# A cross-attention mask carried by the last row of the keys

## The chip, the core and the metric

One core of a Trainium2 chip runs the whole kernel. The time is the device time of one execution, in microseconds; the figure for a kernel is the median of several runs. The profile is of one further execution. The engines are named as the profile names them: PE is TensorE (PEld its weight loads), DVE is VectorE, ACT is ScalarE, POOL is GpSimd, SP is SyncE, which here only issues DMAs.

## What is computed

The input is 8 batches of 256 rows with 128 features, and a context of 64 rows with 64 features for each batch. Four stages follow one another: a memory attention with 16 heads (L0), a small cross-attention (L1), six identical transformer layers (L2), and a last attention with a layer norm (L3). All is in 32-bit floats. Nearly all of the time goes to L2, and the change is in its cross-attention:

```python
def _mha(s, t, kv_w, q_w, o_w, o_b, mask):
    k, v = jnp.split(s @ kv_w, 2, axis=-1)
    q = t @ q_w
    ...
    scores = jnp.einsum('bhqd,bhkd->bhqk', q, k) * D ** (-0.5)
    scores = jnp.where(mask[:, None] == 0, jnp.float32(-1000000000.0), scores)
    attn = jax.nn.softmax(scores, axis=-1)
    ...

def step(t, p):
    tn = _ln(t, norm_g, norm_b)
    t = _mha(tn, tn, skv, sq, sow, sob, tgt_mask) + t     # self-attention, 256 keys
    tn = _ln(t, norm_g, norm_b)
    t = _mha(src, tn, ckv, cq, cow, cob, src_mask) + t    # cross-attention, 64 keys
    tn = _ln(t, pg, pb)
    t = t + (jax.nn.relu(tn @ w1 + b1) @ w2 + b2)
```

`src` is the context, the same in all six layers, and `src_mask` is one row of 64 flags for each batch. 16 heads of 64 features are used.

## The kernel before

The kernel is one long program without loops on the chip. Its order is written out by hand: `at(tick, phase, fn)` puts a step into a plan, and at the end (L1307 to L1323) the plan is gone through by tick and, within a tick, by phase. Every instruction of the four compute engines is tied to stand behind the one before it on its own engine. So on each engine the instructions run in the order of the plan, and an instruction that waits holds up all that stand behind it on its engine. DMAs on SP's queue are not tied in this way.

In each layer self-attention takes four ticks a batch (`plan_sa`), then cross-attention two ticks a batch (`plan_ca`), one for each half of 128 query rows. `T_ca` is the tick at which a layer's cross-attention begins; below, "tick n" of a layer means `T_ca + n`, so batch b has its two score blocks in ticks 2b and 2b+1, for b = 0 to 7. The feed-forward part (`plan_ff`) of batch b stands in ticks 2b+7 and 2b+9, and the next layer's self-attention projections begin in tick 12.

The pieces of cross-attention, each with its line:

- The layer norm runs ahead (`ahead`): statistics on DVE (L849 to L855, phase 6 of tick 2b-4, so in even ticks, where the feed-forward part's statistics of another batch stand too), a power on POOL (L859), the normalising on ACT (L868), a transpose on PE (L882), and a copy out of PSUM on ACT that applies scale and bias of the norm feature by feature (L884). Features are then partitions.
- The weights of queries and keys of all heads are folded together once a layer (`plan_ca_weights`): the weights are transposed on DVE (L1057), written to DRAM and fetched back regrouped (L1060, L1068), regrouped again on POOL (L1074) and multiplied on PE (L1083), which gives `AT` (with the attention's scale, L1095) and `WVO` (L1093). `T_ca - 6` is the tick it is planned from.
- `keys_both` makes the keys of two batches from `AT` and the context (L1120, ticks 4i-2, phase 3.7), copied by ACT into two buffers of the tag "q" (L1126). A key tile is 128 partitions (features of the query side) by 16 heads by 64 keys.
- `plan_weights_64`, one block of 128 query rows by 16 heads by 64 keys. In tick n: `scores` (phase 1) on PE, sixteen 128x32 matmuls (L356) and sixteen mask matmuls (L363); `lower` (phase 2): a copy on ACT (L372), the max on DVE (L374), a subtraction on POOL (L375); the exponents on ACT (L381, phase 8). In tick n+1, the sum and reciprocal on DVE (L385, L386) and the division on POOL (L387), at phase 2.4. In tick n+2 the transposes on DVE (L395, phase 2.5). In tick n+3 the output matmuls on PE (L429, phase 3.0) and the residual add on DVE (L1145).
- Values (L318 on PE, L324 on ACT) come in even ticks, phase 3.2. The feed-forward matmuls (L1161, L1178) come in odd ticks, phases 3.1 and 3.2, and the add behind the second of them (L1182) on DVE.

So within one tick DVE does, in this order, the max of this tick's block, sum and reciprocal of the block before, transposes of the one before that, the residual add of the one before that, and in even ticks statistics.

The mask is a small bf16 array `nm2` whose partition 0 holds 0 or -1e30 for each batch and key, and zeros elsewhere. `ones0` has a one only in partition 0. The mask matmul adds that row to each query row in PSUM:

```python
for a in range(4):
    nc.tensor.matmul(
        sc[32 * a : 32 * a + 32, q, :], lhsT=ones0, rhs=mask,
        start=False, stop=True,
    )
```

In self-attention (`plan_sa`) the names that come up are the scores (L939), the exponents on DVE and ACT (L953, L958), the division on POOL (L968), transposes (L978), output matmuls (L994), the copy of their result by DVE (L299), the value projection (L921), the other projections (L902), the output projection (L1012) and the add behind it (L1019). Outside of layers: L513 and L515 are small DVE instructions of L0's entropy, L631 an add of L1's values, L873 the normalising of self-attention's rows on DVE.

Of the kernel before, what the change touches and what calls it, by code (L numbers as in the profile page):

```python
# [8 lines left out]
F32 = mybir.dt.float32  # L9
# [18 lines left out]
def tile_xattn_stack(ctx: ExitStack, tc: tile.TileContext, io, out: bass.AP):  # L28
# [124 lines left out]

    norm_g = column("L2_norm_g")
    norm_b = column("L2_norm_b")
    pre_g = load_const("L2_pre_gT", [D, NL])
    pre_b = load_const("L2_pre_bT", [D, NL])
    ff_b1 = load_const("L2_ff_b1T", [P, NL, FF // P])
# [103 lines left out]
        return nm  # L262


    nm2 = const.tile([P, B, M], BF16, tag="nm2", name="nm2")
    nc.vector.memset(nm2, 0.0)
    ones0 = const.tile([P, 32], BF16, tag="ones0", name="ones0")
    nc.vector.memset(ones0, 0.0)
    nc.vector.memset(ones0[0:1], 1.0)


    def stats(xin, eps):
# [21 lines left out]
    def at(tick, phase, fn):  # L294
        plan.setdefault(tick, []).append((phase, fn))
# [30 lines left out]
        )  # L326
        return vw

    def plan_weights_64(tick, qt, qT, keys, values, mask, take):

        tl = {}

        def scores():
            sc = two_banks("sc").rearrange("p (q x) -> p q x", q=4)
            if mask is None:
                for i in range(4):
                    for a in range(4):
                        q = (i + 2 * (a // 2)) % 4  # L340
                        rows = slice(64 * (a // 2), 64 * (a // 2) + 64)
                        qb = 4 * qt + q
                        nc.tensor.matmul(
                            sc[32 * a : 32 * a + 32, q, :],
                            lhsT=qT()[rows, qb * 32 : (qb + 1) * 32],
                            rhs=keys()[rows, 4 * (a % 2) : 4 * (a % 2) + 4, :].rearrange(
                                "p h k -> p (h k)"
                            ),
                            start=True, stop=True,
                        )  # L350
                tl["sc"] = sc.rearrange("p q x -> p (q x)")
                return
            for q in range(4):
                qb = 4 * qt + q
                for a in range(4):
                    nc.tensor.matmul(  # L356
                        sc[32 * a : 32 * a + 32, q, :],
                        lhsT=qT()[:, qb * 32 : (qb + 1) * 32],
                        rhs=keys()[:, a].rearrange("p h k -> p (h k)"),
                        start=True, stop=False,  # L360
                    )
                for a in range(4):
                    nc.tensor.matmul(  # L363
                        sc[32 * a : 32 * a + 32, q, :], lhsT=ones0, rhs=mask,
                        start=False, stop=True,
                    )
            tl["sc"] = sc.rearrange("p q x -> p (q x)")

        def lower():
            sc = tl.pop("sc")  # L370
            e = big("e", shape=(P, 16, M))
            nc.scalar.copy(e.rearrange("p h k -> p (h k)"), sc)  # L372
            m = sm([P, 16], "m16")
            nc.vector.tensor_reduce(m, e, AX.X, ALU.max)  # L374
            nc.gpsimd.tensor_tensor(  # L375
                e, e, m.unsqueeze(2).to_broadcast([P, 16, M]), ALU.subtract
            )
            tl["e"] = e

        def exps():  # L380
            nc.scalar.activation(tl["e"], tl["e"], AF.Exp)  # L381

        def divide():
            r = sm([P, 16], "r16")
            nc.vector.tensor_reduce(r, tl["e"], AX.X, ALU.add)  # L385
            nc.vector.reciprocal(r, r)  # L386
            nc.gpsimd.tensor_tensor(  # L387
                tl["e"], tl["e"], r.unsqueeze(2).to_broadcast([P, 16, M]), ALU.mult
            )

        def turn():
            e = tl.pop("e").rearrange("p (q h) (k x) -> p (h k) q x", q=4, x=32)
            eT = big("k" if mask is None else "o", shape=(P, 8, 4, 32))
            for i in range(2):
                nc.vector.transpose(eT[:, 4 * i : 4 * i + 4], e[:, 4 * i : 4 * i + 4])  # L395
            tl["eT"] = eT

        def sums_by_head():

            ps = two_banks("mm").rearrange("p (i x) -> p i x", i=2)  # L400
            eT, vw = tl.pop("eT"), values()
            for i in range(2):
                for k in range(2):
                    for j in range(4):
                        nc.tensor.matmul(
                            ps[32 * j : 32 * j + 32, i, :P],
                            lhsT=cones.rearrange("p a f -> p (a f)") if i == 0
                            else vw[:, 4 * k + j, :],
                            rhs=eT[:, 2 * j + k].rearrange("p q x -> p (q x)"),
                            start=(k == 0), stop=(k == 1),  # L410
                        )
# [12 lines left out]
        def sums():  # L424
            ps = mm_tile()
            eT, vw = tl.pop("eT"), values()
            for s in range(8):
                g, r, k = s // 4, s // 2 % 2, s % 2
                nc.tensor.matmul(  # L429
                    ps[:, :D], lhsT=eT[:, s].rearrange("p q x -> p (q x)"),  # L430
                    rhs=vw[:, r, k, g, :], start=(s == 0), stop=(s == 7),
                )
            take(ps)

        at(tick, 1, scores)
        at(tick, 2, lower)
        if mask is None:
# [197 lines left out]

    def mask_keys():
        mi = big("q", dtype=I32)
        mi = mi[0:1, : B * M].rearrange("p (b m) -> p b m", b=B)
        nc.sync.dma_start(out=mi, in_=io["mask_Bx1xS2_if1"].rearrange("b o m -> o b m"))
        nc.vector.tensor_scalar(nm2[0:1], mi, 0.0, -BIG, ALU.is_equal, ALU.mult)  # L640

    mask_bf = []

# [39 lines left out]
    def plan_l0(b, T):  # L683
# [87 lines left out]
        at(T + 1, 3.2, make_values)  # L771
        for qt in range(QT):
            plan_weights_64(
                T + qt, qt, lambda: st["q"], lambda: st["k"], lambda: st["VW"], None,
                lambda ps, qt=qt: add(qt, ps),
            )
        at(T + 3, 6, moments)
# [268 lines left out]
    def plan_ca_weights(l, T):  # L1046
# [54 lines left out]
            at(T - 4 + i, -0.5, lambda i=i: fetched(i))  # L1101
        at(T + 1, 8.05, regrouped)
        at(T + 2, 3.6, folded("AT", 0, lambda c: st[1][:, :, c, :], HD ** -0.5))
        at(T + 3, 3.6, folded("WVO", 1, lambda c: W["ca", l][2][:, c, :]))

    keys_of = {}

    def plan_ca(l, b, T):
# [3 lines left out]
        def keys_both():  # L1112
# [16 lines left out]
                    )  # L1129
            keys_of[b], keys_of[b + 1] = res  # L1130

        def make_values():
            st["VW"] = values_of(b, fold["WVO"])

        def res():
            st["tb"] = residual(b, W["ca", l][3])

        ahead(b, (T - 4, 6), (T - 3, 2.95), (T - 2, 2.9), norm_g, norm_b, st)
        if b % 2 == 0:
            at(T - 2, 3.7, keys_both)  # L1140
        at(T + 2, 3.2, make_values)
        at(T + 2, 7, res)

        def add(qt, ps):
            nc.vector.tensor_add(t[:, QT * b + qt, :], ps[:, :D], st["tb"][:, qt, :])  # L1145

        for qt in range(QT):
            plan_weights_64(
                T + qt, qt, lambda: st["tT"], lambda: keys_of[b], lambda: st["VW"],
                nm2[:, b].unsqueeze(1).to_broadcast([P, 4, M]), lambda ps, qt=qt: add(qt, ps),  # L1150
            )

    def plan_ff(l, b, T, T_second, steps=None):
# [117 lines left out]
    for l in range(NL):  # L1271
        T_ca = T0 + 4 * B
        T_next = T_ca + 2 * B
        for b in range(B):
            plan_sa(l, b, T0 + 4 * b)
        plan_ca_weights(l, T_ca - 6)
        for b in range(B):
            plan_ca(l, b, T_ca + 2 * b)
            T_ff = T_ca + 2 * b + 7
# [101 lines left out]
```

## Time and profile before

| | |
|---|---|
| median of 3 runs | 2408.54 us (2406.35 to 2409.70) |
| profiled execution, its own time | 2410.29 us |
| profiled execution, span | 2408.5 us |
| mean granted clock of TensorE | 0.987 |
| mask matmuls L363 | 1536 records, 112.4 us busy, 273 ns each |
| score matmuls L356 | 3072 records, 217.0 us busy, 382 ns each |
| max L374, sum L385 (DVE) | 1217 and 1208 ns each |
| subtraction L375, division L387 (POOL) | 1902 ns each |
| ACT waiting for the mask matmuls | 25.4 us, 47 times |

Busy time of a group of matmuls is the time in which at least one of them is under way; up to eight records lie over one another, and a float matmul has two records. The profile's times are microseconds from the start of the span. In a timeline a row is a start, a length, the engine, the line, the operation, output and input, and how many instructions were merged. In the chain of waits each row is a start, a length and the instruction that the end of the program is traced back through.

### The profile page before, as it was taken

The page shows a single profiled execution, that of the slowest core. Times are in us where ns is not written, and L with a number is a line of the kernel's source. Part 1 is how long each engine was busy: PE and PEld are TensorE (multiplying, and loading weights), DVE is VectorE, ACT ScalarE, POOL GpSimd, SP SyncE. Part 2 cuts the span into 40 slices and gives each one's busy share as a digit, 9 for nine tenths or more (in the row PEclk, how much of TensorE's full clock was granted, in tenths as well). Part 3 has the DMA queues.
Part 4 walks back from the last instruction along what each step waited for, and adds up shares of the span by engine and source line. Part 5 has one row for each costly group of instructions (what it writes and reads, how often), then busy time and mean ns, then how long its engine had stood idle before and what let it go on. Part 6 is the DMA issues. An engine that isn't in the chain of part 4 may idle for free.

```text
span 2408.5 us, 100346 instructions
## 1 busy us (share of the span) xinstructions
PE 2325.2 (97%) x42564; PEld 1719.9 (71%) x42564; DVE 1872.3 (78%) x6237; ACT 1707.7 (71%) x4514; POOL 1359.1 (56%) x2231
## 2 busy tenths in 40 slices
PE   7889999999999999999999999999999999999997
PEld 4557777777777777777777777777777777777775
DVE  5677887777888767888767888767888767888775
ACT  4567777667777667778667778667778667777663
POOL 2444556754556754555764555755555765455665
PEclk9989999999999999999999999999999999999998
DMA  6000022001022001012000012000013000001000
GB/s 180 2 2 20 21 73 65 2 3 30 21 64 66 11 3 30 21 56 73 12 2 26 21 45 87 12 2 18 25 40 89 21 2 18 25 26 42 2 4 16
DMA packets 102834, 76.90 MB, mean 32 GB/s; under 512 B 8113, under 2 KB 96881, under 8 KB 102386
## 3 DMA queue, kind: packets, MB, share of 16 engines
q1 hardware_dynamic: 101794, 70.16, 10.1%
q8 instruction: 335, 5.49, 0.9%
q14 instruction: 113, 0.93, 0.1%
q10 hardware_dynamic: 592, 0.33, 0.1%
HBM read 62.07 MB, written 8.39 MB: 29 GB/s over the span
## 4 chain that ended last, share of the span: by engine, by line
PE 75%; DVE 13%; ACT 5%; POOL 4%; issue 2%; DMA 0%; SPq 0%; POOLq 0%; ACTq 0%; DVEq 0%
PE sc L939 12%; PE mm L902 12%; PE mm L994 12%; PE mm L1012 6%; PE mm L921 6%; PE mm L429 6%; PE sc L356 5%; DVE e L953 3%; PE mm L1178 3%; PE mm L1161 3%; DVE eTc L978 2%; DVE m L374 2%; POOL e L968 2%; PE mm L1120 2%; PE mm L318 2%
## 5 line engine op out<-in xcount | busy, mean ns | idle before, releaser
L968 POOL TENSOR_SCALAR e<-e,rs 128x256 f32<-128x256 f32 x1536 | 702.8, 478 | 706.3 <-DVE rs L966 696.5
L958 ACT ACTIVATE e<-e,mn 128x256 f32<-128x256 f32 x1536 | 758.6, 495 | 151.3 <-DVE mn L953 146.5
L953 DVE CUSTOM_DVE_ANT_0 e<-sc,nm 128x256 f32<-128x256 f32 x1536 | 543.1, 419 | 93.4 <-PE sc L939 92.3
L978 DVE STREAM_TRANSPOSE eTc<-e 128x512 f32<-128x512 f32 x768 | 516.2, 694 | 59.4 <-POOL e L968 58.2
L939 PE MATMUL sc<-k,q 64*32 64x256 f32 x12288 | 380.8, 383 | 2.3 <-DVE o L299 1.3
L994 PE MATMUL mm<-eTc,v 32*64 32x256 f32 x12288 | 363.4, 378 | 5.7 <-ACT AT L1095 3.3
L375 POOL TENSOR_TENSOR e<-e,m 128x1024 f32<-128x1024 f32 x112 | 213.0, 1902 | 262.1 <-DVE m L374 262.1
L994 PEld LDWEIGHTS mm<-eTc,v 32*64 32x64 f32 x12288 | 277.1, 131 | 88.5 <-issue 22.2
L939 PEld LDWEIGHTS sc<-k,q 64*32 64x32 f32 x12288 | 221.8, 107 | 125.3 <-issue 51.4
L374 DVE TENSOR_REDUCE m<-e 128x16 f32<-128x1024 f32 x112 | 136.3, 1217 | 197.0 <-ACT e L372 197.0
L958 ACT ACTIVATION_READ_ACCUMULATOR e<-e,mn 128x1 f32 x1536 | 287.9, 187 | 0.0
L356 PE MATMUL sc<-q,tT 128*32 128x256 f32 x3072 | 217.0, 382 | 3.8 <-DVE t L1019 3.2
L429 PE MATMUL mm<-v,o 128*128 128x128 f32 x1536 | 197.5, 283 | 1.9 <-DVE t L1145 1.7
L429 PEld LDWEIGHTS mm<-v,o 128*128 128x128 f32 x1536 | 183.1, 195 | 19.0 <-issue 9.1
L902 PE MATMUL mm<-tT,w_sk 128*128 128x256 f32 x768 | 189.2, 389 | 0.2 <-PE mm L994 0.2
L1012 PEld LDWEIGHTS mm<-w_sow,o 128*128 128x128 f32 x1536 | 175.1, 192 | 17.6 <-issue 12.3
L921 PE MATMUL mm<-w_sv,tT 128*32 128x256 f32 x3072 | 185.6, 382 | 0.0
L1012 PE MATMUL mm<-w_sow,o 128*128 128x128 f32 x1536 | 183.6, 278 | 1.3 <-ACT WVO L1093 1.3
L387 POOL TENSOR_TENSOR e<-e,r 128x1024 f32<-128x1024 f32 x96 | 182.6, 1902 | 0.5 <-DVE r L386 0.5
L301 ACT COPY v<-mm 128x1024 f32<-128x1024 f32 x96 | 97.1, 1012 | 115.4 <-PE mm L921 115.4
L902 PE MATMUL mm<-tT,w_sq 128*128 128x256 f32 x768 | 173.6, 379 | 0.0
L902 PEld LDWEIGHTS mm<-tT,w_sk 128*128 128x128 f32 x768 | 138.3, 190 | 44.2 <-issue 29.2
(222 smaller groups left out, 3489.4 us busy)
## 6 DMA issues: line engine op xcount, KB each, us to landing
nm<-mask_d SPq DMA_DIRECT2D x192, 128.0 KB
wd<-o SPq DMA_DIRECT2D x48, 128.0 KB
w_sk<-in_L_sa_kv_dram SPq DMA_DIRECT2D x6, 512.0 KB
w_sv<-in_L_sa_kv_dram SPq DMA_DIRECT2D x24, 128.0 KB
w_sq<-in_L_sa_q_dram SPq DMA_DIRECT2D x6, 512.0 KB
w_sow<-in_L_sa_ow_dram SPq DMA_DIRECT2D x6, 512.0 KB
w_ckv<-in_L_ca_kv_dram SPq DMA_DIRECT2D x12, 256.0 KB
w_cq<-in_L_ca_q_dram SPq DMA_DIRECT2D x6, 512.0 KB
```

Of the source, the lines that this page charges most:

```text
L356: nc.tensor.matmul(sc[32 * a : 32 * a + 32, q, :], lhsT=qT()[:, qb * 32 : (qb + 1) * 32], rhs=keys()[:, a].rearrange("p h k -> p (h k)"), ...
L375: nc.gpsimd.tensor_tensor(e, e, m.unsqueeze(2).to_broadcast([P, 16, M]), ALU.subtract)
L429: nc.tensor.matmul(ps[:, :D], lhsT=eT[:, s].rearrange("p q x -> p (q x)"), rhs=vw[:, r, k, g, :], start=(s == 0), stop=(s == 7),)
L902: nc.tensor.matmul(ps[:, i * S : (i + 1) * S], lhsT=w[:, c * P : (c + 1) * P], rhs=st["tT"], start=True, stop=True,)
L921: nc.tensor.matmul(ps[32 * a : 32 * a + 32, i, :], lhsT=st["tT"][:, kb * 32 : (kb + 1) * 32], rhs=sv[:, a].rearrange("p g x -> p (g x)"), ...
L939: nc.tensor.matmul(sc[32 * a : 32 * a + 32, r, j, :], lhsT=st["q"][g][rows, a, qb * 32 : (qb + 1) * 32], rhs=st["k"][g][rows, a, :], start ...
L953: nc.vector.tensor_tensor_reduce(e[:, i, :], sc4[:, i, :], st["nm"][:, 2 * jj + i % 2, :], -1.0, 3.0 * BIG, ALU.add, ALU.min, mn[:, i : i ...
L958: nc.scalar.activation(e[:, i, :], e[:, i, :], AF.Exp, scale=-1.0, bias=mn[:, i : i + 1], accum_out=rs[:, i : i + 1],)
L968: nc.gpsimd.tensor_scalar(e[:, i, :], e[:, i, :], rs[:, i : i + 1], 1.0, ALU.mult, ALU.mult)
L978: nc.vector.transpose(eT[:, r, :, 2 * jj : 2 * jj + 2, :], e[:, 2 * r : 2 * r + 2, :].rearrange("p j (k x) -> p k j x", x=32),)
L994: nc.tensor.matmul(ops[a // 2][r * HD : (r + 1) * HD, a % 2, :S], lhsT=st["v"][kb // 4][rows, kb % 4, (2 * g + r) * HD : (2 * g + r + 1) * ...
L1012: nc.tensor.matmul(st["ps"][:, j * D : (j + 1) * D], lhsT=st["oT"][c // 4][:, c % 4, j * P : (j + 1) * P], rhs=sow[:, c, :], start=(c == 0 ...
```

## The change

The mask no longer goes through matmuls. A layer norm's normalised features sum to zero, so the last of the 128 is minus the sum of the others, and its place can be given away: the copy out of PSUM (L884) writes a constant 1 into the last feature, with scale 0 and bias 1 there, and scale 1 and bias 0 elsewhere. The norm's scale and bias move into the folded key weights `AT`: a new set of steps multiplies them by the scale, subtracts the last column from all others, and puts the sum of the products with the bias into the last column. The last row of a key tile then meets the constant 1, and the mask is added to it: one DVE instruction on partitions 96 to 127 for each batch of each layer, with `nm2` now zero except in partition 127. The weight folding is planned one tick earlier, from `T_ca - 7`.

```diff
+    norm_rows = const.tile([P, 2, D], F32, tag="norm_rows", name="norm_rows")
+    for i, name in enumerate(("L2_norm_g", "L2_norm_b")):
+        nc.sync.dma_start(out=norm_rows[:, i, :], in_=io[name].partition_broadcast(P))
...
-    nm2 = const.tile([P, B, M], BF16, tag="nm2", name="nm2")
-    nc.vector.memset(nm2, 0.0)
-    ones0 = const.tile([P, 32], BF16, tag="ones0", name="ones0")
...
+    nm2 = const.tile([P, B, M], F32, tag="nm2", name="nm2")
+    last_on = ident[:, P - 1 : P]
+    last_off = const.tile([P, 1], F32, tag="last_off", name="last_off")
+    nc.vector.tensor_scalar(last_off, last_on, -1.0, 1.0, ALU.mult, ALU.add)
+    last_big = const.tile([P, 1], F32, tag="last_big", name="last_big")
+    nc.vector.tensor_scalar(last_big, last_on, -BIG, None, ALU.mult)
...
                         rhs=keys()[:, a].rearrange("p h k -> p (h k)"),
-                        start=True, stop=False,
-                    )
-                for a in range(4):
-                    nc.tensor.matmul(
-                        sc[32 * a : 32 * a + 32, q, :], lhsT=ones0, rhs=mask,
-                        start=False, stop=True,
+                        start=True, stop=True,
                     )
...
     def mask_keys():
         mi = big("q", dtype=I32)
-        mi = mi[0:1, : B * M].rearrange("p (b m) -> p b m", b=B)
-        nc.sync.dma_start(out=mi, in_=io["mask_Bx1xS2_if1"].rearrange("b o m -> o b m"))
-        nc.vector.tensor_scalar(nm2[0:1], mi, 0.0, -BIG, ALU.is_equal, ALU.mult)
+        mi = mi[:, : B * M].rearrange("p (b m) -> p b m", b=B)
+        nc.sync.dma_start(
+            out=mi, in_=io["mask_Bx1xS2_if1"].rearrange("b o m -> (b o) m").partition_broadcast(P)
+        )
+        nc.vector.tensor_scalar(nm2, mi, 0.0, last_big, ALU.is_equal, ALU.mult)
...
         at(T + 2, 3.6, folded("AT", 0, lambda c: st[1][:, :, c, :], HD ** -0.5))
+
+        def rows(i):
+            return norm_rows[:, i].unsqueeze(1).to_broadcast([P, HC, D])
+
+        def meet_bias():
+            st["z"] = big("q", shape=(P, HC, D))
+            nc.gpsimd.tensor_tensor(st["z"], st["AT"], rows(1), ALU.mult)
+
+        def sum_bias():
+            st["add"] = sm([P, HC], "add")
+            nc.vector.tensor_reduce(st["add"], st.pop("z"), AX.X, ALU.add)
+
+        def scale():
+            nc.gpsimd.tensor_tensor(st["AT"], st["AT"], rows(0), ALU.mult)
+
+        def lose_last():
+            last = sm([P, HC], "last")
+            nc.gpsimd.tensor_copy(last, st["AT"][:, :, D - 1])
+            nc.gpsimd.tensor_tensor(
+                st["AT"], st["AT"], last.unsqueeze(2).to_broadcast([P, HC, D]), ALU.subtract
+            )
+
+        def put_bias():
+            nc.gpsimd.tensor_copy(st["AT"][:, :, D - 1], st.pop("add"))
+
+        at(T + 2, 8.05, meet_bias)
+        at(T + 3, 2.35, scale)
+        at(T + 3, 8.05, lose_last)
+        at(T + 3, 8.7, sum_bias)
+        at(T + 4, -0.1, put_bias)
...
     def plan_ca(l, b, T):
...
+        def mask_keys():
+            last = keys_of[b][96:].rearrange("p a c k -> p (a c) k")
+            nc.vector.tensor_tensor(
+                last, last, nm2[96:, b].unsqueeze(1).to_broadcast([32, 16, M]), ALU.add
+            )
...
-        ahead(b, (T - 4, 6), (T - 3, 2.95), (T - 2, 2.9), norm_g, norm_b, st)
+        ahead(b, (T - 4, 6), (T - 3, 2.95), (T - 2, 2.9), last_off, last_on, st)
         if b % 2 == 0:
             at(T - 2, 3.7, keys_both)
+        at(T - 1, 5, mask_keys)
...
-        plan_ca_weights(l, T_ca - 6)
+        plan_ca_weights(l, T_ca - 7)
```

More of the change, by code (lines that the diff above doesn't have):

```diff
@@ L262, in load_mask @@
         return nm
-    nm2 = const.tile([P, B, M], BF16, tag="nm2", name="nm2")
-    nc.vector.memset(nm2, 0.0)
-    ones0 = const.tile([P, 32], BF16, tag="ones0", name="ones0")
-    nc.vector.memset(ones0, 0.0)
-    nc.vector.memset(ones0[0:1], 1.0)
+    nm2 = const.tile([P, B, M], F32, tag="nm2", name="nm2")
[4 more added lines that the diff above has]
+    nc.vector.tensor_scalar(last_big, last_on, -BIG, None, ALU.mult)
     def stats(xin, eps):
@@ L327, in values_of, with plan_weights_64 @@
         return vw
-    def plan_weights_64(tick, qt, qT, keys, values, mask, take):
+    def plan_weights_64(tick, qt, qT, keys, values, halves, take):
         tl = {}
@@ L336, in scores @@
             sc = two_banks("sc").rearrange("p (q x) -> p q x", q=4)
-            if mask is None:
+            if halves:
                 for i in range(4):
@@ L392, in turn @@
             e = tl.pop("e").rearrange("p (q h) (k x) -> p (h k) q x", q=4, x=32)
-            eT = big("k" if mask is None else "o", shape=(P, 8, 4, 32))
+            eT = big("k" if halves else "o", shape=(P, 8, 4, 32))
             for i in range(2):
@@ L436, in plan_weights_64 @@
         at(tick, 2, lower)
-        if mask is None:
+        if halves:
             at(tick + 1, 2.05, exps)
@@ L773, in plan_l0 @@
             plan_weights_64(
-                T + qt, qt, lambda: st["q"], lambda: st["k"], lambda: st["VW"], None,
+                T + qt, qt, lambda: st["q"], lambda: st["k"], lambda: st["VW"], True,
                 lambda ps, qt=qt: add(qt, ps),
@@ L1149, in plan_ca @@
                 T + qt, qt, lambda: st["tT"], lambda: keys_of[b], lambda: st["VW"],
-                nm2[:, b].unsqueeze(1).to_broadcast([P, 4, M]), lambda ps, qt=qt: add(qt, ps),
+                False, lambda ps, qt=qt: add(qt, ps),
             )
```

## The prediction

> **What bounds the kernel now.** I read the page's busy row first, then the timeline of the first layer's cross-attention (390 to 506 us), then the chain of waits inside it, then the granted clock in 1 us stretches.
>
> ```profile
> PE 2325.2 (97%) x42564; PEld 1719.9 (71%) x42564; DVE 1872.3 (78%) x6237; ACT 1707.7 (71%) x4514; POOL 1359.1 (56%) x2231
> ```
>
> TensorE sets the time in most stages, so the 1536 mask matmuls look like a plain gain. One score block of an odd cross-attention tick, TensorE's rows:
>
> ```profile
> 453.32 0.64 PE L356 MATMUL sc<-q,tT 128*32 128x256 f32 x8
> 453.77 0.29 PE L363 MATMUL sc<-nm,ones 128*32 128x256 bf16 x4
> 453.88 0.61 PE L356 MATMUL sc<-q,tT 128*32 128x256 f32 x8
> ...
> 455.40 0.29 PE L363 MATMUL sc<-nm,ones 128*32 128x256 bf16 x4
> 455.62 2.05 PE L429 MATMUL mm<-v,o 128*128 128x128 f32 x16
> ```
>
> The block takes 453.32 to 455.62 = 2.30 us. Without the mask it looks like the value projection, also sixteen 128x32 float matmuls over 256 columns (two records each), which takes 300.02 to 301.88 = 1.86 us:
>
> ```profile
> 300.02 1.93 PE L921 MATMUL mm<-w_sv,tT 128*32 128x256 f32 x32
> 301.88 1.96 PE L939 MATMUL sc<-k,q 64*32 64x256 f32 x64
> ```
>
> But cross-attention is not bound by TensorE throughout. The chain of waits for ticks 4 to 6 holds VectorE almost alone:
>
> ```profile
> 428.58 0.18 DVE t L1145
> ...
> 431.03 1.12 DVE m L374
> 432.15 1.14 DVE r L385
> ...
> 433.48 1.24 DVE o L395 x2
> 434.72 0.19 DVE t L1145
> ...
> 434.95 2.95 PE mm L429 x16
> ```
>
> VectorE runs a tick behind TensorE: the tick-6 scores ran at 430.17, while VectorE was still at tick 5 (max, sum, transposes, residual add) until 434.89. Today nothing in the scores needs VectorE's latest work. That lead is what the change touches.
>
> **What it removes.** 16 mask matmuls in each of 96 score blocks: 2.30 - 1.86 = 0.44 us a block. If TensorE bound everywhere: 96 x 0.44 = 42 us. (The group's own 112.4 us busy overstates this: the records overlap.)
>
> **What it adds on VectorE.** 48 mask adds, 32x1024 float, both inputs in SBUF. No such row exists; the nearest is the 128x1024 add with one input in PSUM (L631, 1.207 us). With about 0.05 us for the semaphore I take 1.25. Its place decides. In the changed program's order it stands, for every batch b, behind the residual add of tick 2b-1 (behind L1182 where there is one), and the scores of tick 2b read those keys. So the scores of each even tick now wait for max, sum, reciprocal, transposes, add and mask of the tick before. Ends of VectorE's last instruction ahead of the mask, against the start of the even scores, in the trace of before: tick 1 408.52 against 406.24; tick 3 423.53 / 420.39; tick 5 434.89 / 430.17; tick 7 448.95 / 447.54; tick 9 462.29 / 461.11; tick 11 478.61 / 478.39; only tick 13 is early, 497.79 / 498.99. Even with a free mask add TensorE would wait six times of seven.
>
> The waits can't just be added, because in before the same lateness is paid later (tick 6 waits 1.19 + 0.28 us). So I rebuild the distance from one even score start to the next. Pieces from rows: scores to max 3.04 (before 416.10 to 419.56 = 3.46, less 0.44, plus 0.02); max to end of add 3.9 (ticks 3, 5, 7), 4.3 with L1182 (tick 9); an even max to the next with two batches' statistics between 6.15 (424.79 to 430.94); mask 1.25.
>
> | even tick to even tick | before | after | change |
> |---|---|---|---|
> | start: values(0), copy ends 397.46, mask | 396.66 | 398.70 | +2.05 |
> | 0 to 2: 3.04 + 5.23 (max to max through ACT) + 3.17 (max to copy end) + 1.25 | 9.58 | 12.69 | +3.1 |
> | 2 to 4: 8.9 (TensorE) + 3.04 + 3.97 + 1.25 | 14.15 | 17.16 | +3.0 |
> | 4 to 6: 3.04 + 6.15 + 3.9 + 1.25 | 9.78 | 14.34 | +4.6 |
> | 6 to 8: 7.55 (TensorE, with keys) + 3.02 + 3.96 + 1.25 | 17.37 | 15.78 | -1.6 |
> | 8 to 10: 3.04 + 6.14 + 4.29 + 1.25 | 13.57 | 14.72 | +1.2 |
> | 10 to 12: 10.54 (three statistics) + 6.36 + 1.25 | 17.28 | 18.15 | +0.9 |
> | 12 to 14: TensorE, two blocks shorter, mask just fits | 20.60 | 19.77 | -0.8 |
> | 14, 15: two blocks shorter | | | -0.9 |
>
> Sum +11.5 us a layer; six layers **+69 us**. The second layer's starts (765.84, 775.41, 789.56, 799.35, 816.70, 830.27, 847.54, 868.15) have the same distances. Self-attention behind it is full on TensorE (100.00 of 100 us between 200 and 300), so nothing of this is won back there.
>
> **First rule against row: the port.** VectorE and GpSimd:
>
> ```profile
> 46.74 1.90 POOL L375 TENSOR_TENSOR e<-e,m 128x1024 f32<-128x1024 f32 x1 [10.60 <-DVE m L374]
> 48.11 0.81 DVE L513 TENSOR_TENSOR e<-e 8x256 f32<-8x256 f32 x1
> 48.95 0.41 DVE L515 TENSOR_REDUCE lmax<-e 8x1 f32<-8x256 f32 x1
> ```
>
> A product of two SBUF inputs took 0.81 us, twice the one-input instruction of its size beside it, and ended 0.28 us after GpSimd's instruction (48.64). The Trainium skill, "SBUF — State Buffer", section "Who interferes with whom", says why: a VectorE instruction with two SBUF inputs and a GpSimd instruction that reads SBUF exclude each other for a whole instruction. The mask add is of this kind, and GpSimd's 1.90 us division (L387) runs where it would start: until 410.40 (tick 1, starting 20 ns ahead, so half), 424.62, 436.10, 450.05, 463.17, clear in tick 11, 497.99. Waits about 1.0 + 1.1 + 1.2 + 1.1 + 0.8 + 0 + 0.2 = 5.4 us a layer, **+32**. By the L631 row alone the sum is 69, by the rule 101. I take the rule, since L513 shows it here.
>
> **Second: the clock.** After the idle pieces between 432.55 and 434.95 the granted clock fell:
>
> ```profile
> 435.00:436.00 1.00, 1.00 (x9) 1.00 (x10) 0.00 (x0) 1.00 (x2) 1.00 (x1) 0.95 0.00 0
> 436.00:437.00 1.00, 1.00 (x6) 1.00 (x6) 0.74 (x1) 1.00 (x3) 0.10 (x1) 0.50 0.00 0
> ```
>
> (columns: us, busy PE, PEld, DVE, ACT, POOL, clock, DMA). It stayed at half for about 3.4 us, so a fall costs 1.7 us; the output matmuls took 2.95 instead of 2.05. "TensorE: Matmul & The Clock Gate", section "What's actually happening", lets the clock fall after one idle window of about 3.4 us. New idle stretches from the table: 17.16 - 8.9 - 3.84 = 4.4 in tick 3, 14.34 - 5.27 - 3.96 = 5.1 in tick 5, some 4 in tick 1, 1.8 to 2.5 in ticks 7 and 9, plus the port waits. By the rule three falls a layer, by this row (a shorter gap sufficed) up to seven; four of the six layers already have one. I take two net: 2 x 1.7 x 6 = **+20**. Bounds: 0 and 61 (six net).
>
> **The rest.** Per layer GpSimd gets three 128x1024 instructions (1.90 each, L375) and two small copies in self-attention ticks, where it idles 3 us or more before each tick's first division (3.04, 3.11, 3.86); the fold is finished over a tick before the keys need it. Uncovered it would cost 6 us a layer. One VectorE sum (1.21, L385) stands before the exponents of the next tick, where VectorE otherwise waits for scores; bounds 0 and 7 in all, I take **+3**. The moved weight transposes, their DMA writes and fetches keep their spacing one tick earlier, SP's queue stays nearly idle (10.1% of DMA), and w_ckv's next load goes ahead of one mask load: 0. L884 keeps shape and count, with other scale operands: 0. At the start two 64 KB broadcasts stand on SP behind what the first stages need, at about 0.5 us issue each, the mask's load becomes 128 rows wide and its compare 128x512 instead of 1x512: below 1 us, taken as 0.
>
> **Sum.** 69 + 32 + 20 + 3 = 124 us on the profiled execution's 2410.3 (span 2408.5 and 1.8 around it): 2534. The median of the runs is 1.75 below it: **2533 us**.
>
> **Rivals.**
> - *The mask add hides and TensorE gains 42 us: 2367.* For: TensorE is 97% busy, and VectorE idles 2.5 to 2.9 us before each max. Against: this idle lies behind the mask add's place, not in front; it would need VectorE 1.25 us ahead of the even scores, and it is 0.2 to 4.7 behind in six of seven. It decides if the adds really stand clear of the scores. 5%.
> - *Gain and waits cancel: about 2409.* Needs two thirds of the table's waits away. 2%.
> - *The bare chain, no port wait and no clock fall: 69 + 3, 2481.* For: the add's second input is a small repeated row. Against: L513. 25%.
> - *The clock falls after every wait: 69 + 32 + 61 + 7, 2578.* For: this trace's short gap. 12%.
>
> The forecast's case keeps 56%. **Range** 2466 to 2570: from somewhat below the bare chain to most of the clock case. A change of 0.2% (5 us) is what can be told from none: faster 5%, same 2%, slower 93%.
>
> **What would show it.** L356's block at 1.86 us, no L363; waits "PE sc L356 <- DVE" near 2 to 6 us in even ticks, seven a layer; mask adds of 1.2 us where GpSimd is idle and about 2.3 where L387 runs; granted clock 0.5 behind the longest waits; unchanged self-attention ticks. Even scores starting with no wait for VectorE would make the forecast wrong; mask adds all near 1.2 us would take 32 off it.

## The result, and the profile after

The changed kernel takes **2615.57 us** (median of 6 runs, 2594.95 to 2621.89) against 2407.77 (6 runs): a ratio of **1.0843** with a 95% interval of 1.0793 to 1.0893. It is slower, as forecast, but by 208 us where 124 were forecast, and outside the range of 2466 to 2570. The profiled execution is one of the shortest: 2595.18 us, span 2593.5, so 185.0 us over the span of before. The median is 20 us above it; that difference lies between executions, and no trace shows them (last section).

The busy row and the clock's row of the page after:

```profile
PE 2350.3 (91%) x41028; PEld 1715.1 (66%) x41028; DVE 1968.7 (76%) x6290; ACT 1709.5 (66%) x4514; POOL 1428.6 (55%) x2261
...
PEclk8989998899998899999899999899999899999898
```

1536 matmuls are gone (42564 to 41028), and yet TensorE is busy for 2350.3 us where it was 2325.2: the rest ran slower. The mean granted clock went from 0.987 to 0.951, and dips to 8 recur once or more in each layer. VectorE has 96 us more, of which the adds below hold 89, half as much again as the 48 x 1.25 = 60 of the sum.

TensorE in ticks 3 and 4 of the first layer (start, length, instruction; in brackets the idle time ahead of it and what ended it):

```profile
426.99 1.93 PE L362 MATMUL sc<-q,tT 128*32 128x256 f32 x32
428.86 2.05 PE L430 MATMUL mm<-v,o 128*128 128x128 f32 x16
436.44 3.64 PE L362 MATMUL sc<-q,tT 128*32 128x256 f32 x32 [5.54 <-DVE q L1167]
440.02 0.69 PE L885 MATMUL tp<-ident,xn 128*128 128x128 f32 x2
```

The odd tick's block takes 1.87 us from its start to the next instruction's (426.99 to 428.86), where it took 2.30: the mask is gone from it as meant. The even block then waits 5.54 us for the mask add (L1167), and its row is 3.64 us long where the odd one's is 1.93, with no instruction added. The granted clock around it, in 1 us stretches (columns: length in us, busy PE, PEld, DVE, ACT, POOL, then the clock, DMA's share and GB/s):

```profile
433.00:434.00 1.00, 0.00 (x0) 0.00 (x0) 1.00 (x3) 0.61 (x1) 1.00 (x2) 0.94 0.00 0
434.00:435.00 1.00, 0.00 (x0) 0.00 (x0) 0.97 (x2) 0.45 (x1) 1.00 (x1) 0.50 0.00 0
...
439.00:440.00 1.00, 1.00 (x12) 0.21 (x4) 0.00 (x0) 0.00 (x0) 0.00 (x0) 0.50 0.00 0
440.00:441.00 1.00, 1.00 (x10) 0.98 (x7) 0.00 (x0) 0.86 (x1) 0.00 (x0) 0.65 0.00 0
```

The clock fell some 3 us into the wait, before the block began, and came back only behind it. VectorE in the same tick, and below it GpSimd:

```profile
430.16 1.22 DVE L375 TENSOR_REDUCE m<-e 128x16 f32<-128x1024 f32 x1 [3.59 <-ACT e L373]
...
432.70 1.24 DVE L396 STREAM_TRANSPOSE o<-e 128x512 f32<-128x512 f32 x2
433.87 0.25 DVE L1185 TENSOR_TENSOR t<-mm,tb 128x128 f32<-128x128 f32 x1
434.15 2.15 DVE L1167 TENSOR_TENSOR q<-q,nm 32x1024 f32<-32x1024 f32 x1
```

```profile
433.31 1.90 POOL L388 TENSOR_TENSOR e<-e,r 128x1024 f32<-128x1024 f32 x1
```

The add could start at 434.15 and should take 1.22; it takes 2.15. It ended 1.1 us after GpSimd's division did (435.21). All the adds together, min/median/max in ns:

```profile
L1167 DVE TENSOR_TENSOR q<-q,nm x48: 1221/1864/2952, 400.1 to 2526.7; 32x1024 f32<-32x1024 f32 x48
```

They sum to 89.3 us, 30.7 over 48 x 1.22. And the waits list has TensorE behind them 43 times:

```profile
PE sc L362 <- DVE q L1167: 166.1, 43, 6.6
```

Where the 185 us are, from the starts of the even score blocks (first layer of each; the others agree to within about 1.5 us but for the last layer):

| stretch | before | after | the fill run below, its lowest | the prediction's table with its port waits |
|---|---|---|---|---|
| tick 0 to 2 | 9.58 | 14.55 | 14.55 | 13.7 |
| 2 to 4 | 14.15 | 20.10 | 18.26 | 18.3 |
| 4 to 6 | 9.78 | 17.29 | 15.48 | 15.5 |
| 6 to 8 | 17.37 | 18.61 | 16.69 | 16.9 |
| 8 to 10 | 13.57 | 17.44 | 15.48 | 15.5 |
| 10 to 12 | 17.28 | 18.05 | 18.15 | 18.2 |
| 12 to 14 | 20.60 | 21.50 | 19.88 | 20.0 |
| sum | 102.3 | 127.5 | 118.5 | 118.1 |
| tick 14 to the next layer's tick 0 | 266.85 | 271.84 | 271.9 | |

Over six layers the stretches hold 155.9 us of the 185.0; the five gaps between layers 25.1, the start of the first layer 5.1, and the end gives 1.1 back.

### The profile page after: what moved, and what is told of

It is laid out like the page before. It is cut to its first block, busy times and chain, and to the rows that moved or that the text cites. A ratio compares the mean times of both kernels' runs of the same rounds, so it can differ in the third digit from the quotient of the medians.

```text
span 2593.5 us, 97367 instructions
## 1 busy us (share of the span) xinstructions
PE 2350.3 (91%) x41028; PEld 1715.1 (66%) x41028; DVE 1968.7 (76%) x6290; ACT 1709.5 (66%) x4514; POOL 1428.6 (55%) x2261
## 4 chain that ended last, share of the span: by engine, by line
PE 75%; DVE 15%; ACT 4%; POOL 4%; issue 2%; DMA 0%; POOLq 0%; ACTq 0%; DVEq 0%
PE sc L942 13%; PE mm L905 12%; PE mm L997 12%; PE sc L362 7%; PE mm L924 7%; PE mm L1015 6%; PE mm L430 5%; DVE q L1167 3%; PE mm L1218 3%; PE mm L1201 3%; DVE m L375 2%; PE tp L885 2%; POOL e L971 2%; PE mm L324 2%; DVE o L396 2%
## 5 line engine op out<-in xcount | busy, mean ns | idle before, releaser
L971 POOL TENSOR_SCALAR e<-e,rs 128x256 f32<-128x256 f32 x1536 | 706.3, 484 | 671.4 <-DVE rs L969 661.7
L997 PE MATMUL mm<-eTc,v 32*64 32x256 f32 x12288 | 373.2, 385 | 13.2 <-ACT WVO L1096 9.7
L362 PE MATMUL sc<-q,tT 128*32 128x256 f32 x3072 | 232.1, 453 | 166.6 <-DVE q L1167 166.1
L997 PEld LDWEIGHTS mm<-eTc,v 32*64 32x64 f32 x12288 | 283.3, 134 | 99.7 <-issue 18.8
L362 PEld LDWEIGHTS sc<-q,tT 128*32 128x32 f32 x3072 | 109.9, 126 | 257.9 <-issue 167.7
L373 ACT COPY e<-sc 128x1024 f32<-128x1024 f32 x112 | 113.5, 1013 | 210.0 <-PE sc L362 183.7
```

Source lines behind the costliest of these rows:

```text
L362: nc.tensor.matmul(sc[32 * a : 32 * a + 32, q, :], lhsT=qT()[:, qb * 32 : (qb + 1) * 32], rhs=keys()[:, a].rearrange("p h k -> p (h k)"), ...
L971: nc.gpsimd.tensor_scalar(e[:, i, :], e[:, i, :], rs[:, i : i + 1], 1.0, ALU.mult, ALU.mult)
L997: nc.tensor.matmul(ops[a // 2][r * HD : (r + 1) * HD, a % 2, :S], lhsT=st["v"][kb // 4][rows, kb % 4, (2 * g + r) * HD : (2 * g + r + 1) * ...
```

## The experiments

Times are medians, ratios against the kernel before (2408.2 to 2408.7 in these runs), with the 95% interval. "The change" is the changed kernel. Five of the runs compute something else: the change without its add, that again with the folding not moved and with it spread, and the kernel before without its mask matmuls leave the mask out (in this input no key is masked, so it would have added zeros); and the run with one input puts a transposition of the key rows in the add's place. The line numbers of some runs differ from the change's by a few.

**The add ahead of the max.** Is it the add, or the add's place?

```diff
-        at(T - 1, 5, mask_keys)
+        at(T - 1, 1.9, mask_keys)
```

> The mask add stands at phase 1.9 instead of 5 of the same tick, ahead of the max. Place theory (the add itself is cheap, its place behind max, sum, transposes and residual add makes the even scores wait, and the waits make the clock fall): no even score block waits for the add, the cross-attention falls behind before by the 42 us of the mask matmuls, some 10 to 15 us come back in the ticks where VectorE has no idle time before the max, and the fold still costs about 25: 2395 to 2420 us. Rival (the add costs by its own length and by the port it shares with GpSimd, wherever it stands): above 2520 us.

Measured: **2436.85** (2432.94 to 2438.67), 1.012 [1.0102, 1.0137]. One number in the order takes away 179 of the 207 us. Against the run without any add (next), the same 48 instructions on the same data cost 26 us here and 205 where the change has them: the cost is the place. The expected 2395 to 2420 was missed, and the run shows where. The waits for the add are down to 13.6 us, and all six are in tick 6.

```profile
437.18 3.28 PE L362 MATMUL sc<-q,tT 128*32 128x256 f32 x32 [2.26 <-DVE q L1167]
```

There the add of b = 3 stands behind two batches' statistics, which leave VectorE no idle time ahead of the max:

```profile
435.62 0.16 DVE L858 TENSOR_SCALAR mneg<-mv 128x2 f32<-128x2 f32 x1
435.81 1.22 DVE L1167 TENSOR_TENSOR q<-q,nm 32x1024 f32<-32x1024 f32 x1
437.07 1.22 DVE L375 TENSOR_REDUCE m<-e 128x16 f32<-128x1024 f32 x1
```

The larger part of the 26 us lies behind it. In tick 11 the add of b = 6 stands behind three batches' statistics, and TensorE's waits for VectorE's normalised rows (L876) are 16.1 us in all, against 6.4 in the run without any add. In the first layer ticks 10 to 12 take 19.32 us (17.08 without adds) and 12 to 14 take 21.34 (19.73), the latter with a clock fall in it.

**No add, and the two halves of the rest.** First the change without its add:

```diff
-        at(T - 1, 5, mask_keys)
```

> The mask add is left out (all keys of this input are valid, so it adds zeros); the folding stays. Place theory and port theory both: the waits go, about 2408 - 42 + 20 to 30 for the fold = 2385 to 2396 us. If the cross-attention stays slow without the add, its cause is another (the folding, or the copy out of PSUM): above 2450.

Measured: **2410.70** (2408.61 to 2415.72), 1.0011 [1.0005, 1.0018]. That is above the 2385 to 2396 expected: with no mask at all, neither by matmul nor by add, the changed kernel is no faster than before. So something besides the add eats the gain. Two runs split it. First the kernel before without its mask matmuls:

```diff
-                        start=True, stop=False,
-                    )
-                for a in range(4):
-                    nc.tensor.matmul(
-                        sc[32 * a : 32 * a + 32, q, :], lhsT=ones0, rhs=mask,
-                        start=False, stop=True,
+                        start=True, stop=True,
                     )
```

> The kernel before without its mask matmuls, nothing else changed (the mask is left out; all keys of this input are valid). 0.44 us in each of 96 score blocks if TensorE binds everywhere: 2366 us. If VectorE's chain in ticks 3 to 6 binds instead, part of it is lost: 2380 to 2390.

Measured: **2388.64** (2387.75 to 2391.26), 0.9923 [0.9908, 0.9937]. TensorE loses 1536 matmuls, which would be 42 us if it set the time everywhere; 20 come off. From tick 4 to 6 the distance goes from 9.78 to 9.73: VectorE's chain there does not care. So the most that this change could have gained was 20 us, 0.8%.

Then the change without its add and with the lines of the diff above put back, that is the folding alone, with the mask in matmuls as before:

> The change with the mask matmuls put back and the mask add left out: only the folding, its move by a tick and the constant last feature remain. The prediction's value for these was 3 us: 2411. What the stretch between two cross-attentions shows in the changed kernel (271.8 against 266.9 us, and 401.8 against 396.7 at the start, of which some 2.4 wait for the add) is 2.5 to 3.5 us a layer: 2423 to 2430.

Measured: **2431.26** (2430.00 to 2431.97), 1.0097 [1.0082, 1.0112]. The folding costs **22.5 us** (2431.26 - 2408.73), and 22.1 by the other pair (2410.70 - 2388.64). The prediction had 3. TensorE in the last self-attention ticks ahead of the first layer's cross-attention, before:

```profile
376.28 0.66 PE L994 MATMUL mm<-eTc,v 32*64 32x256 f32 x8 [0.17 <-ACT AT L1095]
...
384.72 0.44 PE L882 MATMUL tp<-ident,xn 128*128 128x128 f32 x2
385.38 3.84 PE L1012 MATMUL mm<-w_sow,o 128*128 128x128 f32 x32 [0.22 <-ACT WVO L1093]
```

and with the folding alone:

```profile
378.15 0.66 PE L1007 MATMUL mm<-eTc,v 32*64 32x256 f32 x8 [1.25 <-ACT WVO L1106]
...
385.91 0.71 PE L895 MATMUL tp<-ident,xn 128*128 128x128 f32 x2 [1.16 <-ACT xn L881]
386.91 5.46 PE L1025 MATMUL mm<-w_sow,o 128*128 128x128 f32 x32 [0.28 <-ACT o L312]
```

The product for WVO has moved up a tick with the rest of the plan; the output matmuls behind it now wait 1.25 us for ACT to copy it, the transposes wait 1.16 for ACT's normalised rows, and after these pieces the projection takes 5.46 instead of 3.84, with the granted clock at 0.50 from 388 to 391 us. But the slowed projection is not what the folding costs. Ahead of the fifth layer no fall comes and it takes 3.84; TensorE waits 1.25, 1.15, 0.27 and 1.00 us there, and that gap between layers (271.28 us) is no shorter than the others (270.24 to 270.29; before, 266.84 to 266.99). What sets the gap is GpSimd. The chain of waits of the changed kernel ahead of its second layer holds two of the added products, the scale (L1120) and the subtraction of the last column (L1125), between divisions (L971) that self-attention waits for:

```profile
775.22 1.84 POOL e L971 x4
777.06 2.33 POOL AT L1120
779.39 1.83 POOL e L971 x4
781.21 0.15 POOL last L1124
...
781.44 1.90 POOL AT L1125
783.33 0.67 POOL rstd L862
...
784.40 1.83 POOL e L971 x4
```

From the first division of one tick to that of the next 9.2 us pass (775.22 to 784.40), where before it was 6.7 (744.14 to 750.84). Ahead of the first layer the same two stand on the chain, at 377.69 and 382.06; before, no GpSimd step of the folding does. Two runs ask whether the earlier tick or GpSimd's steps are at fault.

**The folding not moved**, no add:

```diff
-        at(T - 1, 5, mask_keys)
...
-        plan_ca_weights(l, T_ca - 7)
+        plan_ca_weights(l, T_ca - 6)
```

> No mask add (it would add zeros), and the folding planned from T_ca - 6 as before instead of T_ca - 7, with its new steps. The run without the add took 2410.7, the kernel before without its mask matmuls 2388.6, so the folding and its move cost 22. If the move by a tick is the cost (the copy of the folded values late, TensorE waiting for it, a clock fall behind it): 2390 to 2397. If GpSimd's new instructions are the cost wherever they stand: 2408 to 2414.

Measured: **2396.03** (2393.35 to 2399.68), 0.9949 [0.9934, 0.9963]: 14.7 of the 22 come back, and the wait for WVO with them. The 7.4 that stay (2396.03 - 2388.64) go with a new wait, for the last step of the folding:

```profile
PE mm L1153 <- POOL AT L1130: 10.4, 6, 1.7
```

**The folding moved, but GpSimd's steps spread over three ticks**, no add:

```diff
-        at(T + 3, 2.35, scale)
-        at(T + 3, 8.05, lose_last)
+        at(T + 3, 8.05, scale)
+        at(T + 4, 8.05, lose_last)
...
-        at(T + 4, -0.1, put_bias)
+        at(T + 5, -0.1, put_bias)
```

> No mask add, the folding from T_ca - 7, but its three long GpSimd instructions spread over three ticks, one behind each tick's last division: scale moves from phase 2.35 to 8.05 of its tick, the subtraction of the last column one tick later. If scale's place between the two divisions of a tick is the cost: 2392 to 2400. If the move by a tick is: about 2408 to 2412.

Measured: **2398.86** (2397.13 to 2400.57), 0.9958 [0.9941, 0.9974]. This gets 11.8 back, with the tick moved, and no fall in that place. TensorE there:

```profile
378.55 0.66 PE L997 MATMUL mm<-eTc,v 32*64 32x256 f32 x8 [1.25 <-ACT WVO L1096]
...
385.26 0.71 PE L885 MATMUL tp<-ident,xn 128*128 128x128 f32 x2
386.25 3.84 PE L1015 MATMUL mm<-w_sow,o 128*128 128x128 f32 x32 [0.28 <-ACT o L307]
```

The wait for WVO is still there, since the tick is; the wait for ACT is gone, since one long product instead of two now stands in that tick, ahead of the small products that ACT's normalising needs (L862, L865); and the projection takes 3.84 again. The subtraction stands in the next tick, and TensorE waits 5.6 us in all for the last step behind it (L1153 for L1130, six times). The two remedies win back 14.7 and 11.8 of 22 us, more than there is: the cost is neither the earlier tick alone nor GpSimd's products alone, but the two meeting in one tick. How much either would cost by itself is not told apart.

**The port.** The mask add reads two SBUF inputs. Here a transposition of the same rows, which reads one, stands in its place:

```diff
-            nc.vector.tensor_tensor(
-                last, last, nm2[96:, b].unsqueeze(1).to_broadcast([32, 16, M]), ALU.add
-            )
+            last = keys_of[b][96:].rearrange("p a c k -> p (a c k)")
+            nc.vector.transpose(last, last)
```

> In the mask add's place stands an instruction of like length with one input: a transpose in 32x32 blocks of the same 32 rows of the keys, in place (the mask is left out and the last 32 rows of the keys are permuted, so the scores are others). Port theory: each takes about 1.2 us wherever GpSimd is; the changed kernel's 48 adds waited 89.3 - 48 x 1.22 = 30.7 us in all, so it ends 25 to 35 us earlier, about 2580 to 2590 at the median. Rival (the wait at the port lies beside the chain, the place and the clock make all of it): no change, 2600 to 2620.

Measured: **2573.71** (2571.65 to 2574.63), 1.0684 [1.0668, 1.07]. The instruction's length no longer varies at all:

```profile
L1167 DVE STREAM_TRANSPOSE q<-q x48: 1241/1241/1243, 401.2 to 2501.7; 32x1024 f32<-32x1024 f32 x48
```

So the spread from 1.22 to 2.95 us is the second SBUF input beside GpSimd's division, as the Trainium skill has it in "SBUF — State Buffer", section "Who interferes with whom". Span against span the run is 20.6 us shorter (2593.5 to 2572.9), where the adds had lost 30.7 in length; by the medians it is 41.9, with the changed kernel's longer executions in it. The 25 to 35 expected lie between. The trace has 35 clock falls in cross-attention ticks, the changed kernel's 31, so covered waits and added falls are not told apart. The prediction's 32 for the port is right in length; this pair leaves its effect between 20 and 42.

**The clock.** Dummy matmuls (128x512) fill TensorE's idle time ahead of the even scores, 18 in each layer, everything else as in the change:

```diff
+        if b > 0:
+            at(T - 1, 8.9, lambda: fill((0, 4, 4, 5, 3, 1, 1, 0)[b]))
```

> The changed kernel with 18 more 128x512 float matmuls a layer (ident times the context, into a PSUM tile that nobody reads), put in the plan just before the even scores, 4, 4, 5, 3, 1, 1 and 0 of them in ticks 1 to 13: TensorE works through most of each wait. Clock theory: the clock no longer falls in the cross-attention; six falls of 1.78 us a layer go, about 60 us: 2535 to 2560 us, granted clock near 0.98, and runs that lie closer together than 2595 to 2622. Rival (the slow scores aren't the clock's doing, or the time is all in the waits themselves): no earlier than before, 2600 or more, since TensorE has 18 x 6 matmuls more to do.

Measured: **2564.94** (2562.75 to 2571.46), 1.0653 [1.0636, 1.0671], with 100 us of useless matmuls in it, and 5 above the 2535 to 2560 expected. TensorE does more, and the span is 30.5 us shorter (2593.5 to 2563.0), the granted clock 0.978 instead of 0.951. The even block of tick 4 again:

```profile
432.00 3.60 PE L1175 MATMUL mm<-ctx,ident 128*128 128x512 f32 x8
437.70 1.93 PE L362 MATMUL sc<-q,tT 128*32 128x256 f32 x32 [2.10 <-DVE q L1167]
```

It still waits for the add, but runs in 1.93 us. Where the clock holds, the distances are those in the table's fourth column: 9.0 us a layer below the change, and within 0.2 us of the prediction's chain and port but for tick 0 to 2. Some ticks of some layers still have a fall (17.0 where 15.48 is had elsewhere), 12 in cross-attention ticks where the change has 31, which is why 30.5 and not 54 us are won.

**Adds placed one by one.** Can a masked kernel beat both? Each add goes to a tick with idle time on VectorE ahead of the max; keys 6 and 7 are made two ticks earlier for it.

```diff
-            at(T - 2, 3.7, keys_both)
-        at(T - 1, 5, mask_keys)
+            at(T - (4 if b == 6 else 2), 3.7, keys_both)
+        at(T + (-1, -1, -1, -3, -1, -2, -2, -1)[b], 1.9, mask_keys)
```

With the folding spread as above (and WVO a tick later):

> The whole change, with each mask add ahead of a max that VectorE reaches early: for b = 0 to 7 in ticks -1, 1, 3, 3, 7, 8, 10, 13 at phase 1.9, the keys of batches 6 and 7 made two ticks earlier, the folding spread over three ticks as in the run with the fold spread, and the values' half of it left in its old tick. Place theory: adds nearly free, the run without mask matmuls (2388.6) plus 3 to 8 for the folding and 2 to 8 for the adds: 2394 to 2405 us, faster than before. Rival (every add costs its 1.2 us wherever it stands, as the early place seemed to show with 26 us for 48): 2415 or more.

and with the folding not moved:

> The same places for the adds and the keys, with the folding as the change has it but planned from T_ca - 6 as before. Place theory: 2396 (that folding without adds) plus 2 to 8: 2398 to 2404 us, faster than before. Rival: 2420 or more.

Measured: **2426.33** (2426.24 to 2427.82), 1.0076 [1.0063, 1.009], and **2412.86** (2409.25 to 2417.26), 1.002 [1.0013, 1.0027]. Both miss. Of the 13.4 us between their spans some 8 lie ahead of the first scores of the layers (gaps of 269.23 us against 267.84), so the spread folding with its later WVO is not the better one here. In the second layer of the latter the stretches 0 to 8 are close to those without an add (9.58, 13.71, 9.72, 15.77), so b = 3's add is cured; but 8 to 10 is 15.12 instead of 13.13, and 12 to 14 is 21.14 instead of 19.73 (10 to 12 gives 0.6 back). The last of these is a clock fall: in the fifth layer, which has none there, 12 to 14 takes 19.73. I took the add of b = 6 in tick 10, with its three statistics, for the cause, and moved it to tick 9, then b = 5's to tick 7 as well:

> Theory: in the run with placed adds, what is left of the cost is the seventh batch's add (b = 6). It stands in tick 10, whose VectorE work already holds three batches' statistics, and the run lost 2.0 us from tick 11 to 12 and 1.4 us from 12 to 13 of each layer against the same fold without adds. With this add in tick 9, ahead of the max, where VectorE has 0.4 us idle and the tick behind it 1.8 us of room: those 3.4 us come back in five layers (the last layer has no next layer's statistics), 2412.9 - 17 = 2396, range 2392 to 2404, below the kernel before. Rival: any add of 1.25 us on VectorE in ticks 8 to 11 costs the same, since that stretch is VectorE's chain: unchanged, 2408 to 2417.

> As the run before, and the sixth batch's add (b = 5) too is one tick earlier, in tick 7, beside the fifth's. Theory: tick 8's max then starts with more room, but tick 7's max, which had no idle time ahead of it (0 us between add and max), starts 1.25 us later; the 2.2 us of idle ahead of tick 8's max take that up: the same as the run before within 3 us, about 2396. Rival (VectorE's chain in ticks 7 to 9 decides): 1.25 us a layer more, 2404.

Measured: **2413.12** (2408.64 to 2415.70), 1.002 [1.0011, 1.0029], and **2416.41** (2414.77 to 2417.41), 1.0035 [1.0021, 1.0049]. No change: with b = 6's add out of tick 10, the stretches are still 15.12, 16.33 and 21.37. That theory falls, and the rows point to the keys instead. TensorE of the second layer without adds (folding not moved), where the keys stay in tick 10:

```profile
827.89 2.06 PE L1153 MATMUL mm<-ctx,AT 64*128 64x128 f32 x32
830.43 1.93 PE L362 MATMUL sc<-q,tT 128*32 128x256 f32 x32 [0.48 <-DVE t L1184]
...
838.85 0.30 PE L885 MATMUL tp<-ident,xn 128*128 128x128 f32 x1 [0.99 <-DVE xn L876]
...
839.70 1.93 PE L362 MATMUL sc<-q,tT 128*32 128x256 f32 x32
```

and with the adds placed and the keys in tick 8:

```profile
823.06 2.06 PE L1153 MATMUL mm<-ctx,AT 64*128 64x128 f32 x32
825.04 1.93 PE L362 MATMUL sc<-q,tT 128*32 128x256 f32 x32
...
847.88 0.30 PE L885 MATMUL tp<-ident,xn 128*128 128x128 f32 x1 [2.79 <-DVE xn L876]
...
848.88 3.35 PE L362 MATMUL sc<-q,tT 128*32 128x256 f32 x32
```

In tick 10 the key matmuls lie beside VectorE's statistics and cost TensorE nothing (the scores of tick 11 even wait 0.48 behind them for VectorE). In tick 8 nothing covers them: 2.0 us. And tick 11, which VectorE sets, now has 2.79 us idle in one piece, after which the scores take 3.35. No run has the adds of b = 6 and 7 without early keys and with b = 3's add cured, so this reading is drawn from the rows and not tested alone. The early-add run speaks for it: with the keys in tick 10 and an add in tick 9 its ticks 8 to 10 take 13.14, as without adds. A masked kernel below 2408 was not found.

## Why the prediction was right, and why it was too low

- **What bounds the kernel** (TensorE in most stages, VectorE's chain in ticks 4 to 6): right. With the mask matmuls simply gone, 20 us come off, not 42, and none in ticks 4 to 6.
- **The chain, +69, and the port, +32**: right, tick by tick (ticks 0 to 2, where the port was a coin's toss, came out 0.9 higher: the add of tick 1 took 2.95). Inside the layers the two bring 102.3 us to 118.1 by the prediction, and to 118.5 by the fill run's lowest distances. The early-add run shows that the place of the add is what costs, the one-input run that the port is what stretches it.
- **The clock, +20: the step that failed.** It read "I take two net: 2 x 1.7 x 6 = +20", with a bound of 61 for six. The trace has five falls in each of the first four layers (ticks 2, 4, 6, 8 and 12), six in the fifth and five in the last, with one in tick 0 in both: 31. The fill run shows those of the first layer worth 9.0 us (1.84 + 1.81 + 1.92 + 1.96 + 1.62, less 0.1 in ticks 10 to 12), so about 54 in six layers. Two faults made five into two. First, the port's waits were named beside the idle stretches and not added to them: the 1.8 to 2.5 us foreseen for tick 7 became 3.81, above the 3.4 that the Trainium skill, "TensorE: Matmul & The Clock Gate", section "What's actually happening", gives for one window. By that rule and the waits of the first layer (5.32, 5.54, 6.31, 3.81 against 2.41 and 1.94 without a fall) it is four a layer. As a rule of length it does not hold in this trace: tick 12 has a fall without such a wait, tick 0 has one in two layers after 2.40 us, and tick 8 of the last layer has none after 3.69. Second, the falls of before were set off against the new ones; but the table of distances was built from pieces without any fall, so there was nothing to set off.
- **The rest, +3: failed too.** The step named the cover on GpSimd, "where it idles 3 us or more before each tick's first division". Only one of the three long products lies in such an idle stretch (L1113, at 772.04 ahead of the second layer); the other two lie on the chain of waits, 2.33 and 1.90 us long, and delay the divisions. The folding costs 22 us. That the moved steps "keep their spacing one tick earlier" was weighed for the DMAs, and not for TensorE, ACT and GpSimd: with the tick not moved, 14.7 of the 22 come back. Two of the three GpSimd products also took 2.36 us rather than the 1.90 of the row they were priced by.
- **The sum.** 69 + 32 + 54 + 22 = 177 gives 2587 beside the profiled 2595. The rival "the clock falls after every wait" (2578, 12%) came nearest, with six falls a layer for five, and its 7 for the folding was still short.
- **The signs named beforehand** came out: L362's block at 1.87 us, waits of 1.4 to 6.3 in seven even ticks of the first layer, adds of 1.2 where GpSimd is idle and 2.2 where it divides. "Unchanged self-attention ticks" did not: each gap between layers is 5.0 us longer, where the table has about 1.2 for the start and ticks 14 and 15.

## What to carry to other kernels

An instruction that takes work off the busiest engine is worth its place in the order, not its length: the same 48 adds cost 205 us behind the residual add and 26 ahead of the max. When a new wait is priced, add all the stretches of it together first (chain and port), and then price the clock for each wait that may bring a fall, on top of a sum that holds no falls. And a plan that moves one tick earlier is to be costed on every engine whose instructions move with it, not only on the one that gets new work.

## What was not expected of the hardware

- The clock also falls after idle time in pieces: in tick 12 of the first layer TensorE idled 1.02, 0.29 and 1.44 us with short transposes between; the clock went to 0.50 at 509.0 us, 1.2 us into the scores behind, and they took 2.59.
- The same wait can bring a fall or not. The 2.40 us ahead of tick 0 leave the block at 1.93 us in four layers and make it 2.62 and 2.56 in the last two; in the last layer 3.69 us ahead of tick 8 leave it at 1.93, and 2.86 ahead of tick 12 make it 3.64. In the trace all falls begin at whole multiples of 3.413 us from one another: in the first layer's cross-attention at 413.4, 433.9, 450.9, 471.4 and 509.0 us, 6, 5, 6 and 11 times 3.413 apart. The fall at 413.4 came 2.4 us into its wait, the one at 450.9 came 3.5 us into it. So it seems to be the place of a wait on this grid that decides; no run here moved a wait alone to test it. The first four layers have their falls at the same ticks, and one layer takes 399.4 us, which is 117 times 3.413.
- The port holds GpSimd back too. In the early-add run its small product L865 took 1.06 us beside a mask add and 0.20 elsewhere:

```profile
436.03 1.06 POOL L865 TENSOR_TENSOR nm<-mneg,rstd 128x2 f32<-128x2 f32 x1
437.81 0.20 POOL L865 TENSOR_TENSOR nm<-mneg,rstd 128x2 f32<-128x2 f32 x1
```

- GpSimd's products with the norm's row repeated over the heads took 2.36 us (six of each, 2361 to 2375 ns); the subtraction with a column repeated along each row, of the same size, 1.90.
- What stays open: the six executions of the changed kernel lie near 2595, 2609 and 2622 with a mean clock of 0.951 to 0.947, where the kernel before holds within 4 us. The clock is lower in the longer ones (0.947 and 0.948 against 0.951), so further falls are likely in them, perhaps because their waits meet the grid at other places; the one trace of this kernel is of a short one and cannot show it.
